# The end of a graph-attention kernel: the last node blocks in groups of 4, 2 and 3, and two steps of the pending work for each pair of edges in the last three blocks

## The chip, the cores and the metric

The kernel runs on one core of a Trainium2 chip. The metric is the device time in microseconds (us) of one execution. PE is the matrix engine (TensorE, with PEld for its weight loads), DVE the vector engine, ACT the scalar engine, POOL GpSimd, which here issues the indirect gathers and scatters, and SP the engine whose queue carries the plain DMAs. Each engine takes its instructions strictly in the order in which the program lists them, and waits on semaphores that the others raise.

## The reference, cut to what matters

There are 6250 nodes of 512 floats and 100,000 edges, each with eight bias values. A layer norm is followed by attention with 8 heads over each node's incoming edges, a projection and a residual, and then by a small "ALU" pipeline: three matrix layers on features decoded from each node's second layer norm, of which two outputs per position are used.

```python
q, k, v = x @ Wq + bq, x @ Wk + bk, x @ Wv + bv      # x is layer-normed, 8 heads of 64
logits = einsum('ehd,ehd->eh', q[rows] * scale, k[cols]) + att_bias
att = softmax of logits over the edges of one row
y = segment_sum(att[:, :, None] * v[cols], rows)
x1 = x + (y @ Wo + bo)
...
h = relu(relu(x_ge @ W0 + b0) @ W1 + b1) @ W2 + b2    # once with Wa, once with Ws
...
out = layernorm(x1) + x1, with a few columns (128 to 160) added to from rounded h
```

(The lines are shortened from the reference; the last stage selects between the two pipelines by flags in columns 0 to 2 of the normed row.)

## The kernel before, in words

The edges are sorted by node on the chip, keys and values of all nodes are written to a table in HBM, and then a main loop handles 49 blocks of 128 nodes (`NB` = 49). Block numbers in this document are places in the loop's order, 0 to 48. A node sits on one partition; a block has as many edge slots as its busiest node has edges (`CAP`): 16 slots in block 45, and 10, 9 and 8 in the last three blocks, 46, 47 and 48. A block of more than 12 slots is taken in two parts.

For each pair of slots POOL gathers two rows of keys and values (`kv`, 4 KB for each partition and slot, 11 buffers of a pair each), and DVE multiplies the keys by the block's query and sums by head (`dots`, L813 and L814, 2.4 us for a pair). After the last pair of a part comes the softmax (L742 to L760, DVE and ACT). The weighting of the values and their sum belong to `sums` (L1091): DVE multiplies the values of most pairs by the softmax's weights (L824), ACT those of the last one or two full pairs (L822, eight short instructions for a slot), and PE adds all slots up with a multiplication by the identity into `p_y` (L1104). `sums` is put off: it is written into the program after the `dots` of the next part's first pair, so for block b it stands behind the first pair of block b+1.

What follows on the sums is a generator for each block, `part_end` (L1058): it divides by the softmax's denominator (L785 to L789), turns the result (L832 on PE, L835 on ACT), multiplies by Wo (L841, L842 on PE), adds the residual and takes mean and variance (L845 to L848 on DVE). The query of the next block is a generator too (`project`: L802 on PE, L804 on ACT, L808 and L809 on PE). When all blocks of a group have come so far, the group's ALU pipeline, the generator `alu` (L850), is put into the list `alus`:

- an "E" step: the square root on ACT (L855) between two table loads, then the norm on DVE and ACT (L858 to L868);
- a "D" step: decoding on DVE (L874 to L887), and a turn on PE (L891); then `fT` is copied out on DVE (L895);
- ten "P" steps on PE and ACT: five matrix products L905 with ACT's relu L907, five outputs of the second layer L918 (13 products) with L920, and then the third layer L925 (5 products). All of them have 128 times the number of blocks in the group as their columns;
- two more "D" steps: `yf` is copied out on DVE (L928), turned back on PE (L932), and DVE makes the outputs (L938 to L973). POOL then scatters one block's rows at a time (L794).

The order of all this is the program's own and fixed when it is built: the scheduler is switched off (`manual_schedule`). `pump` (L1003) is called once ahead of each pair's `dots`: it moves every generator in `going` (`part_end`, `project`) by one step, and `alus` by up to `n` steps of the kinds allowed. `alu_steps` (L1014) does the latter alone; it is called after each softmax for up to four "P" steps. Groups are taken from `alus` one after the other. The groups have 4 blocks; `heads_of` (L1044) cuts the end into groups of 2, 2 and 1: blocks 44 and 45, 46 and 47, and 48. Scatters are held back while gathers remain (`HOLD`, L1130), so all those of blocks 40 to 48 stand behind the last gather. After the last block, the loop at L1160 pumps until nothing is left.

Of the kernel before, what the change touches and what calls it, by code (L numbers as in the profile page):

```python
# [20 lines left out]
P = 128  # L21
# [7 lines left out]
GB = 4  # L29
# [14 lines left out]
def gnn_ffn_kernel(  # L44
# [4 lines left out]
    N, D = x.shape  # L49
# [6 lines left out]
    NB = -(-N // P)  # L56
# [52 lines left out]
    def gather(dst_t, table, idx):  # L109
        nc.gpsimd.indirect_dma_start(  # L110
            out=dst_t, out_offset=None, in_=table,
            in_offset=bass.IndirectOffsetOnAxis(ap=idx, axis=0))
# [111 lines left out]
    def fetch_keys(b):  # L224
        C = CAP[ORDER[b]]
        t, nbuf = ("0", 1) if b == 0 else ("", LA + 3)
        kg = pre.tile([P, C + 1], F32, tag="kg" + t, name="kg", bufs=nbuf)
        gather(kg, words, pos_i[:, ORDER[b]:ORDER[b] + 1])
        st[b] = dict(kg=kg)

    def read_keys(b):
        C = CAP[ORDER[b]]
        t, nbuf = ("0", 1) if b == 0 else ("", LA + 3)
        f0 = pre.tile([P, 1], F32, tag="f0", name="f0", bufs=2)
        neg, eid = decode(st[b]["kg"], 1, C, f0, t, nbuf, ids=nid[:, b:b + 1])
        rec = pre.tile([P, C, ROW], F32, tag="rec" + t, name="rec", bufs=min(nbuf, LA + 2))
        st[b].update(neg=neg, rec=rec, eid=eid)
# [10 lines left out]
    def fetch_recs(n, last):  # L248

        while fetched[0] < n and fetched[1] is not None and fetched[1][0] <= last:  # L250
            b, s = fetched[1]
            gather(st[b]["rec"][:, s, :], rec_d, st[b]["eid"][:, s:s + 1])
            fetched[:] = fetched[0] + 1, next(wanted, None)
# [484 lines left out]
    def softmax(lg, rec, neg, m0):  # L738


        n = lg.shape[1]
        nc.vector.scalar_tensor_tensor(lg, lg, SCALE, rec[:, :, 1:], op0=OP.mult, op1=OP.add)  # L742
        nc.vector.tensor_tensor(lg, lg, neg[:, :, None].to_broadcast([P, n, H]), op=OP.add)
        m = ap_.tile([P, H], F32, tag="m", name="m", bufs=4)
        nc.vector.tensor_reduce(m, lg.rearrange("p c h -> p h c"), AX.X, OP.max)
        if m0 is None:
            nc.vector.tensor_scalar(m, m, FLOOR, None, op0=OP.max)
        else:
            nc.vector.tensor_tensor(m, m, m0, op=OP.max)
        nc.vector.tensor_tensor(lg, lg, m[:, None, :].to_broadcast([P, n, H]), op=OP.subtract)  # L750
        nc.scalar.activation(lg, lg, AF.Exp)  # L751
        turn_[1] ^= 1
        p_ps = pp[:, turn_[1] * P:turn_[1] * P + n * H].rearrange(
            "p (c h) -> p c h", h=H)
        nc.scalar.copy(p_ps, lg)
        cor = None
        if m0 is not None:
            cor = ap_.tile([P, H], F32, tag="cor", name="cor", bufs=3)
            nc.vector.tensor_tensor(cor, m0, m, op=OP.subtract)
            nc.scalar.activation(cor, cor, AF.Exp)  # L760
        return m, cor, p_ps
# [36 lines left out]
    def project(xg, s_):  # L798

        pt = ops.tile([P, KC, P], F32, tag="tr", name="tr", bufs=1)  # L800
        for c in range(KC):
            nc.tensor.transpose(pt[:, c, :], xg[:, D + c * P:D + (c + 1) * P], ident)  # L802
        xT = o2.tile([P, KC, P], F32, tag="xT", name="xT", bufs=2)
        nc.scalar.copy(xT, pt)  # L804
        yield
        q = s_["q"] = ops.tile([P, D], F32, tag="q", name="q")
        for c in range(KC):
            nc.tensor.matmul(q, xT[:, c, :], wq[:, c, :], start=(c == 0), stop=False)  # L808
        nc.tensor.matmul(q, ones3, bq3, start=False, stop=True)  # L809

    def dots(kvt, n, q, dot, s):
        k = kvt[:, :n, :D]
        nc.vector.tensor_tensor(k, k, q[:, None, :].to_broadcast([P, n, D]), op=OP.mult)  # L813
        nc.vector.tensor_reduce(  # L814
            dot[:, s:s + n, :], k.rearrange("p s (h d) -> p s h d", h=H), AX.X, OP.add)
# [164 lines left out]
    def fetch_nodes(b):  # L980
        if b - 4 in ends:
            run(ends.pop(b - 4))
        xg = ap_.tile([P, 2 * D], F32, tag="xg", name="xg", bufs=4)
        gather(xg, xx_d, nid[:, b:b + 1])
        st[b]["xg"] = xg
# [13 lines left out]
    def store(n=1):  # L999
        for _ in range(n):  # L1000
            stores.pop(0)[1]()

    def pump(kinds="", n=1):  # L1003

        last[1] += 1
        for g in list(going):
            if next(g, True):
                if g in going:
                    going.remove(g)
        alu_steps(kinds, n)  # L1010
        if stores and stores[0][0] + last[0] <= last[1]:
            store()

    def alu_steps(kinds, n):  # L1014

        while alus and n > 0 and kind[0] in kinds:
            kind[0] = next(alus[0], None)
            if kind[0] is None:
                alus.pop(0)
                kind[0] = "P"  # L1020
            n -= 1

    def run(g):

        while alus and g in alus and g is not alus[0]:
            run(alus[0])
        for _ in g:
            pass
        if g in alus:
            kind[0] = "P"  # L1030
        for l in (going, alus):
            if g in l:
                l.remove(g)
# [7 lines left out]
                LASTR if ORDER[g + j] == NB - 1 else P), g))  # L1041


    heads_of = list(range(0, NB - 5, GB)) + [NB - 5, NB - 3, NB - 1]  # L1044
    head = {b: max(g for g in heads_of if g <= b) for b in range(NB)}

    def start_group(g):
        i = heads_of.index(g)
        n = (heads_of + [NB])[i + 1] - g
        t, nbuf = ("", 2) if i < len(heads_of) - 2 else (str(i), 1)  # L1050
        if i > 1 and nbuf > 1 and heads_of[i - 2] in groups:
            run(groups.pop(heads_of[i - 2])[2])
            while stores and stores[0][2] <= heads_of[i - 2]:
                store()
        groups[g] = [o2.tile([P, n if t else GB, D], F32, tag="x1" + t, name="x1", bufs=nbuf),
                     o2.tile([P, GB, 2], F32, tag="mv", name="mv", bufs=4), None]
# [55 lines left out]
    for b in range(NB):  # L1112
        C = CAP[ORDER[b]]
        s_ = st[b]
        rec, q = s_["rec"], s_["q"]
        parts = -(-C // PART)
        m = None
        for i in range(parts):
            s0, s1 = C * i // parts, C * (i + 1) // parts
            n_ = s1 - s0  # L1120
            dot = ap_.tile([P, n_, H], F32, tag="dot", name="dot", bufs=2)
            kvs = []
            for s in range(s0, s1, 2):
                n = min(2, s1 - s)
                kvt = kvp.tile([P, 2, 2 * D], F32, tag="kv", name="kv")
                for j in range(n):
                    gather(kvt[:, j, :], kv_d, rec[:, s + j, 0:1].bitcast(I32))
                kvs.append((kvt, n, s - s0))
                done = sum(SLOTS[:b]) + s + n
                if done > HOLD:  # L1130
                    last[0] = 1000
                fetch_recs(FIRST + (TOTAL - FIRST) * done // (TOTAL - LAST), b + LA)
                if s == s0 and i == 0:
                    if b + LA + 2 < NB:
                        fetch_keys(b + LA + 2)
                    if b + 1 < NB:
                        fetch_nodes(b + 1)
                if s == s0 + 2 and i == 0 and b + 1 < NB:
                    pj = project(st[b + 1]["xg"], st[b + 1])
                    going.insert(0, pj)  # L1140


                k = len(kvs) - 1
                pump("" if k < 2 else "D" if s + 2 >= s1 else "DE" if k == 2 else "DEP")
                dots(kvt, n, q, dot, s - s0)
                if s == s0:
                    for f in waiting:
                        f()
                    waiting.clear()
                if s == s0 + 2 and i == parts - 1 and b + LA + 2 < NB:  # L1150
                    read_keys(b + LA + 2)
            m, cor, p_ps = softmax(dot, rec[:, s0:s1], s_["neg"][:, s0:s1], m)
            waiting.append(partial(sums, b, i, parts, dot, cor, p_ps, kvs, n_))
            alu_steps("P", min(4, len(kvs) - 1))
        if b + 1 < NB:
            run(pj)
    for f in waiting:
# [149 lines left out]
```

## Time and profile before

| what | us |
|---|---|
| median of 3 runs (lowest, highest) | 3293.85 (3280.11, 3300.85) |
| the profiled execution, its own time | 3294.45 |
| its span, first to last instruction | 3292.6 |
| main loop's last gather of keys and values issued by POOL (ends) | 3166.9 |
| last `p_y` product of block 48 ends | 3212.5 |
| last DVE instruction (L973 of block 48) ends | 3276.6 |
| busy: PE, DVE, ACT, POOL | 2066.8, 2021.9, 880.8, 1708.2 |
| mean granted clock of PE | 0.800 |

How it is read: times in the trace are us from the span's start. A timeline line has the start, the busy time, the engine, the source line, the operation, what it writes and reads, how many instructions are merged in it, and in brackets how long the engine sat idle before and what released it. A product of 512 columns in f32 is two records of 0.43 us each at PE's full clock. In a table of stages, "PEclk" is the share of PE's clock that was granted. In the records the clock is at either 1.0 or 0.5.

### The profile page before, as it was taken

How to read it: one execution, taken by the hardware profiler on the slowest of the kernel's cores; microseconds unless marked ns; L12 is line 12 of the kernel's file. 1: busy time of each engine (PE TensorE's matmuls, PEld its weight loads, DVE VectorE, ACT ScalarE, POOL GpSimd, SP SyncE). 2: the span in 40 equal slices, each digit the busy share in tenths (PEclk: the TensorE clock that was granted, in tenths of full speed). 3: DMA queues.
4: the chain of work that ended last, by engine and by line, in shares of the span. 5: the costliest groups of instructions: out<-in, count | busy, mean ns of one | idle time of the engine just before them, and what ended most of it. 6: DMA issues, size and time to landing. Idle time of an engine off the chain costs nothing.

```text
span 3292.6 us, 20197 instructions
## 1 busy us (share of the span) xinstructions
PE 2066.8 (63%) x4853; PEld 888.6 (27%) x4853; DVE 2021.9 (61%) x3593; ACT 880.8 (27%) x2656; POOL 1708.2 (52%) x1858
## 2 busy tenths in 40 slices
PE   7887318644556647466477485757757557566586
PEld 3443103311222222122222132222323222222233
DVE  9887000176747655575677558767677766666672
ACT  6443003121212122131232222323223232222232
POOL 2011760274666555655665646665666646656530
PEclk9999658866777878778788788787978879778797
DMA  8443113465555554655565646665666646556530
GB/s 272 170 155 108 25 16 128 142 215 189 171 172 182 161 180 154 200 162 167 186 193 171 200 150 197 196 194 177 195 196 194 203 128 201 186 163 193 164 116 17
DMA packets 193964, 542.30 MB, mean 165 GB/s; under 512 B 51831, under 2 KB 53174, under 8 KB 193841
## 3 DMA queue, kind: packets, MB, share of 16 engines
q0 software_dynamic: 154416, 464.27, 44.9%
q1 hardware_dynamic: 39425, 76.67, 6.7%
q8 instruction: 42, 0.69, 0.1%
q14 instruction: 81, 0.66, 0.1%
HBM read 472.60 MB, written 68.22 MB: 164 GB/s over the span
## 4 chain that ended last, share of the span: by engine, by line
PE 40%; DVE 18%; another core or an unknown queue 17%; issue 16%; ACT 5%; POOL 2%; DMA 1%; SPq 0%; POOLq 0%; DVEq 0%; ACTq 0%
PE p_y L1104 13%; PE pm L468 8%; DVE kv L813 5%; PE pm L918 4%; PE q L808 4%; PE pm L841 3%; DVE dot L814 3%; ACT kv L822 3%; DVE kv L824 3%; PE pm L905 2%; PE p L925 2%; DVE key L143 1%; POOL kv L110 1%; DVE key L144 1%
## 5 line engine op out<-in xcount | busy, mean ns | idle before, releaser
L110 POOL DMA_INDIRECT kv<-kv_d,rec x804 | 760.7, 946 | 763.7 <-PE p_y L1104 346.3
L1104 PE MATMUL p_y<-kv,ident 128*128 128x512 f32 x1608 | 832.9, 674 | 383.5 <-issue 169.6
L110 POOL DMA_INDIRECT rec<-rec_d,eid x804 | 762.8, 949 | 245.1 <-issue 236.6
L813 DVE TENSOR_TENSOR kv<-kv,q 128x1024 f32<-128x1024 f32 (+1 forms) x425 | 489.9, 1153 | 200.1 <-DMA kv<-kv_d,rec 127.5
L1104 PEld LDWEIGHTS p_y<-kv,ident 128*128 128x128 f32 x1608 | 335.3, 215 | 852.2 <-issue 554.2
L814 DVE TENSOR_REDUCE dot<-kv 128x16 f32<-128x1024 f32 (+1 forms) x425 | 493.8, 1162 | 79.2 <-ACT kv L822 42.1
L822 ACT ACTIVATE kv<-kv,dot 128x64 f32<-128x64 f32 x1568 | 387.0, 336 | 31.8 <-issue 31.8
L808 PE MATMUL q<-wq,xT 128*128 128x512 f32 x392 | 215.4, 700 | 271.3 <-issue 185.8
L824 DVE TENSOR_TENSOR kv<-kv,pp 128x1024 f32<-128x1024 f32 (+1 forms) x327 | 352.7, 1137 | 0.0
L841 PE MATMUL pm<-wo,yT 128*128 128x512 f32 x392 | 213.4, 695 | 204.4 <-issue 125.5
L468 PE MATMUL pm<-wv,xnT 128*128 128x512 f32 (+1 forms) x392 | 190.7, 622 | 17.5 <-issue 17.5
L468 PE MATMUL pm<-wk,xnT 128*128 128x512 f32 (+1 forms) x392 | 189.3, 625 | 0.0
L804 ACT COPY xT<-tr 128x512 f32<-128x512 f32 x49 | 28.7, 585 | 594.9 <-remote 333.3
L808 PEld LDWEIGHTS q<-wq,xT 128*128 128x128 f32 x392 | 83.3, 224 | 374.0 <-issue 283.9
L841 PEld LDWEIGHTS pm<-wo,yT 128*128 128x128 f32 x392 | 85.6, 227 | 315.8 <-issue 231.3
L835 ACT COPY yT<-tr 128x512 f32<-128x512 f32 x49 | 28.7, 585 | 482.3 <-remote 262.6
L766 DVE TENSOR_REDUCE den<-dot 128x8 f32<-128x64 f32 (+6 forms) x91 | 24.7, 272 | 198.5 <-ACT dot L751 166.8
L479 ACT COPY kvt<-pm 128x512 f32<-128x512 f32 (+1 forms) x98 | 57.1, 583 | 323.3 <-remote 133.7
L417 DVE RECIPROCAL rstd<-rstd 128x7 f32<-128x7 f32 (+4 forms) x9 | 1.7, 186 | 214.5 <-ACT rstd L413 158.6
L110 POOL DMA_INDIRECT xg<-xx_d,nid x49 | 46.2, 943 | 160.6 <-DMA kv_d<-kvt 128.9
L905 PE MATMUL pm<-fT,w 8*128 8x512 f32 (+2 forms) x140 | 91.0, 774 | 52.1 <-DVE fT L895 28.0
L920 ACT ACTIVATE h<-pm,b 128x512 f32<-128x512 f32 (+2 forms) x70 | 44.1, 633 | 285.3 <-PE pm L918 115.4
(257 smaller groups left out, 2129.1 us busy)
## 6 DMA issues: line engine op xcount, KB each, us to landing
kv_d<-kvt SPq DMA_DIRECT2D x48, 512.0 KB
rec<-rec_d,eid POOLq DMA_INDIRECT x804
kv<-kv_d,rec POOLq DMA_INDIRECT x804
xt<-in_x_dram SPq DMA_DIRECT2D x48, 256.0 KB
xx_d<-xt SPq DMA_DIRECT2D x48, 256.0 KB
xx_d<-xn SPq DMA_DIRECT2D x48, 256.0 KB
rec_d<-R SPq DMA_DIRECT2D x3, 882.0 KB
bt<-in_edge_attr_dram SPq DMA_DIRECT2D x3, 686.0 KB
```

Of the source, the lines that this page charges most:

```text
L110: nc.gpsimd.indirect_dma_start(out=dst_t, out_offset=None, in_=table, in_offset=bass.IndirectOffsetOnAxis(ap=idx, axis=0))
L468: nc.tensor.matmul(pm[:r], xnT[b][:, c, :r], wkv[nm_][:, c, :], start=(c == 0), stop=(i == 1 and c == KC - 1))
L808: nc.tensor.matmul(q, xT[:, c, :], wq[:, c, :], start=(c == 0), stop=False)
L813: nc.vector.tensor_tensor(k, k, q[:, None, :].to_broadcast([P, n, D]), op=OP.mult)
L814: nc.vector.tensor_reduce(dot[:, s:s + n, :], k.rearrange("p s (h d) -> p s h d", h=H), AX.X, OP.add)
L822: nc.scalar.mul(v[:, i, h], v[:, i, h], p[:, s + i, h:h + 1])
L824: nc.vector.tensor_tensor(v, v, p_ps[:, s:s + n, :, None].to_broadcast([P, n, H, DK]), op=OP.mult)
L841: nc.tensor.matmul(pm, yT[:, c, :], wo[:, c, :], start=(c == 0), stop=False)
L905: nc.tensor.matmul(pm[:, :nt], w0[:, c * P:(c + 1) * P], fT[:, t0:t1], start=True, stop=True)
L918: nc.tensor.matmul(pm[:, :nt], w, h1[:, k, :nt], start=(i == 0), stop=(i == len(terms) - 1))
L925: nc.tensor.matmul(p3[:, :nt], w2[:, c, :], h2[:, c, :nt], start=(c == 0), stop=(c == NC4))
L1104: nc.tensor.matmul(p_y, ident, kvt[:, j, D:], start=(done_ == 0), stop=(done_ == n_ - 1))
```

## The change

It does two things, both of which only concern the program after the first pair of block 46.

1. `heads_of` ends with two heads instead of three, so that blocks 46, 47 and 48 are one group of three. Their ALU pipeline runs once with 384 columns, instead of once with 256 and once with 128.
2. In the last three blocks `pump` is called twice ahead of each pair, each time with up to two ALU steps of any kind. `part_end` and `project` so move by two steps for each pair. Before, the first pair allowed no ALU step, the second and last few kinds, and the others one step. After the softmax of these blocks up to four ALU steps of any kind may follow, instead of "P" alone.

```diff
-    heads_of = list(range(0, NB - 5, GB)) + [NB - 5, NB - 3, NB - 1]
+    heads_of = list(range(0, NB - 5, GB)) + [NB - 5, NB - 3]
...
-        t, nbuf = ("", 2) if i < len(heads_of) - 2 else (str(i), 1)
+        t, nbuf = ("", 2) if i < len(heads_of) - 1 else (str(i), 1)
...
                 k = len(kvs) - 1
-                pump("" if k < 2 else "D" if s + 2 >= s1 else "DE" if k == 2 else "DEP")
+                if b >= NB - 3:
+                    pump("DEP", 2)
+                    pump("DEP", 2)
+                else:
+                    pump("" if k < 2 else "D" if s + 2 >= s1 else "DE" if k == 2 else "DEP")
                 dots(kvt, n, q, dot, s - s0)
...
             waiting.append(partial(sums, b, i, parts, dot, cor, p_ps, kvs, n_))
-            alu_steps("P", min(4, len(kvs) - 1))
+            alu_steps("P" if b < NB - 3 else "DEP", min(4, len(kvs) - 1))
```

The second line gives the last group a tile of its own (of 3 blocks instead of one of 2 and one of 1), which leaves the memory used the same.

What the two programs list on PE, one beside the other, from the second part of block 45 on (x counts products; "ALU" with the group's blocks; the third layer is L925):

| before | after |
|---|---|
| ALU 40-43: L905 x3 | ALU 40-43: L905 x5, L918 x4 |
| `p_y` 45, second part, x8; L802 and `q` of 47 | `p_y` 45 x8; L802 of 47; L918 x4; `q` of 47 |
| ALU 40-43: L905 x2, L918 x6 | ALU 40-43: L918 x5, L925 x5, L932 |
| L832 of 45 | L832 of 45; Wo of 45 |
| `p_y` 46 x10; L802 of 48; Wo of 45; `q` of 48 | `p_y` 46 x10; L802 of 48; ALU 44-45: L891, L905 x1; `q` of 48 |
| ALU 40-43: L918 x7, L925 x5; L832 of 46 | ALU 44-45: L905 x4, L918 x4; L832 of 46; L918 x4; Wo of 46; L918 x5, L925 x5, L932 |
| `p_y` 47 x9; Wo of 46; L932 | `p_y` 47 x9; L832 and Wo of 47 |
| `p_y` 48 x8; then L832 and Wo of 47 and 48 among ALU 44-45 | `p_y` 48 x8; L832 and Wo of 48 |
| ALU 46-47; ALU 48 | ALU 46-48, 384 columns |

On DVE, the copy `yf` (L928) of ALU 40-43 stands before in the middle of block 47's pairs, and after behind the second pair of block 46, ahead of the other three. L928 of ALU 44-45 stands before at the end, and after ahead of block 47's last pair (its single slot). POOL's gathers keep their order.

## The prediction

> **What bounds the kernel now.** I read the stage table first, to see where the changed part lies and which engine is busy there; then the timelines of DVE, ACT and PE from 3120 us on; then the chain of waits for the end. Main loop and sort stand in the same order in both programs, so only what follows about 3127 us can differ: 165 of 3292.6 us.
>
> Stages from the table. Columns: stretch, its length, busy us (and instructions) of PE, PEld, DVE, ACT and POOL, PE's granted clock, share of the DMA engines' time, GB/s.
>
> ```profile
> 3121.00:3157.00 36.00, 30.86 (x69) 12.45 (x69) 35.10 (x44) 9.54 (x27) 17.23 (x18) 0.91 0.48 147
> 3157.00:3203.00 46.00, 36.70 (x92) 14.91 (x90) 24.39 (x51) 13.39 (x46) 11.09 (x12) 0.93 0.25 84
> 3203.00:3213.00 10.00, 9.24 (x21) 4.17 (x21) 7.46 (x21) 7.76 (x22) 0.37 (x1) 0.79 0.10 39
> 3213.00:3277.00 64.00, 48.53 (x172) 30.12 (x171) 17.22 (x82) 23.07 (x45) 3.95 (x5) 0.79 0.05 17
> ```
>
> Until 3157 DVE is busy 35.1 of 36 us. From there PE and DVE take turns, and the last 64 us are one chain: the ends of blocks 47 and 48, then three ALU pipelines in a row, DVE 17 us busy and PE 49. The DVE timeline shows the hand-overs that cost:
>
> ```profile
> 3164.49 0.69 DVE L789 TENSOR_TENSOR y<-p_y,den 128x512 f32<-128x512 f32 x1 [6.75 <-PE p_y L1104]
> ...
> 3183.54 0.68 DVE L928 COPY yf<-p 8x512 f32<-8x512 f32 x1 [1.09 <-PE p L925]
> ...
> 3195.95 0.19 DVE L948 TENSOR_TENSOR ys<-py,b 128x32 f32<-128x32 f32 x1 [8.60 <-PE py L932]
> ...
> 3276.43 0.20 DVE L973 TENSOR_TENSOR x<-x,de 128x33 f32<-128x33 f32 x1
> ```
>
> With 1.67 and 2.02 us of smaller waits, DVE stands still 20 us between 3121 and 3203. L928 of the group of four costs it 1.09 us only, because it stands where the pipeline is already through. From ACT and PE:
>
> ```profile
> 3149.07 0.69 ACT L920 ACTIVATE h<-pm,b 128x512 f32<-128x512 f32 x1 [4.29 <-issue]
> 3156.78 1.26 ACT L920 ACTIVATE h<-pm,b 128x512 f32<-128x512 f32 x2 [7.03 <-PE p_y L1104]
> ```
>
> ```profile
> 3146.64 1.02 PE L918 MATMUL pm<-h,w1lm 128*128 128x512 f32 x2
> 3152.17 7.03 PE L1104 MATMUL p_y<-kv,ident 128*128 128x512 f32 x16
> 3203.76 8.79 PE L1104 MATMUL p_y<-kv,ident 128*128 128x512 f32 x16 [7.85 <-DVE kv L824]
> 3242.75 4.83 PE L905 MATMUL pm<-fT,w 8*128 8x256 f32 x10 [0.51 <-DVE fT L895]
> 3255.28 2.33 PE L925 MATMUL p<-h,w 128*8 128x256 f32 x10
> ```
>
> ACT takes at 3156.78 what PE had done at 3147.66: 9 us late, while gathers run at 0.48 of the DMA engines' time. PE's results reach ACT late in such stretches.
>
> **The change, part by part.** All times are of the one profiled execution (3294.45 us, span 3292.6); the difference found is then put on the median of 3293.85, 0.6 below.
>
> *The group of three at the end.* Before, from the end of block 48's last product (3212.55) to the end of the last L973 (3276.63): 64.1 us. After: L789 0.75; turn on PE 0.65; copy on ACT 0.5; Wo 3.95 (3.60 and 0.38 in the rows of 3191); L845 to L848 1.6; the root 0.35, its table load done before; L858 to L863 0.33 and three of L866 0.86; L874 to L887 between 1.25 (two blocks) and 2.1 (four), taken 1.5; turn 0.5; fT 0.55: 11.5 us. PE's 23 products: with 256 columns they took from 3242.75 to 3257.61, 14.9 us; at full clock 46 records of 0.2155 are 9.9, so 5.0 went to a slow clock at the start and to one wait for ACT. With 384 columns 46 x 0.323 = 14.9, and the same 5.0: 19.9. Then yf to L973, 3.2 for two blocks: 3.3. Sum 34.7, **29.4 less**. Three scatters instead of one stand at the end; POOL's pitch for them is 1.27 (3261.11, 3262.38): **2.5 more**. The 16 us behind the last L973 stay.
>
> The Trainium skill ("TensorE: Matmul & The Clock Gate", "What's actually happening") says that the array runs at half rate only for about the first 3.4 us of sustained work; by it the extra would be 1.7, and the sum 3.3 lower. But the granted clock was 0.53 from 3243 to 3252 and 0.99 only from 3252 to 3262: 9 us at half rate, which are 4.5 lost. I keep the row.
>
> *Two steps for each pair.* It moves the rest of ALU 40-43 into block 46's first two pairs, and ALU 44-45 into blocks 46 and 47, both ahead of work that DVE could do. Nothing is computed more; what counts is where L928 comes.
>
> First stall. PE's list is now L905 x5, L918 x4, p_y, L802, L918 x4, q, L918 x5, L925 x5 before L928 can go. The first three L905 end at 3127.7 as before. Two more at half clock with their relus on ACT, and two outputs of L918 at 1.9 each: 3135.9 (before, p_y began at 3127.6). p_y 7.0, L802 0.4, L918 x4 3.7, q 3.9, L918 x5 4.3, L925 4.4: **3159.7**. DVE has done pair 1, three weightings, L845 to L848, L1063 and pair 2 by 3132.7, and stands at L928 for **27 us**; behind it in its queue are three pairs of block 46, the softmax that ACT waits for, all weightings of blocks 46 to 48. Before, it had gone on at once.
>
> From 3159.7: yf and what follows 3.65 (0.6 + 0.83 + 2.25), L1067 to L789 1.84, three pairs 7.15, softmax 1.3, L845 to L848 1.56, ALU 44-45's E step 1.5, one pair and L766 2.65, one weighting 1.15: block 46's p_y can start at 3180.5 (before 3152.2). PE: 20 records of 0.43 are 8.6. PE had waited 9 us; p_y of 48, which came after a wait of 7.85, took 8.79 where 16 records otherwise take 7.03, so 1.8 more: 3191. Turns and fT 1.3, L905 and q 4.6, four L905 2.3, two L918 outputs 1.8, L832 0.5, two outputs 1.8, Wo 4.0, the last output and L925 4.3: L928 of ALU 44-45 at **3211.5**. DVE got there at 3200.8: second stall, 10.7. In front of it, fT waited 6.8 for the turn that stands behind p_y.
>
> Then 3.3 for its outputs, block 47's single slot and softmax 2.7, L845 to L848 1.6, one pair, L766 and a weighting 3.8: p_y 47 starts at 3222.9, 18 records and 1.8 for the clock, 3232.5. L789 0.7, two pairs 4.8, softmax, ACT's exp and L766 1.85, a weighting 1.15: p_y 48 starts at 3241 and ends at **3248.1**, 35.6 later than before.
>
> Sum: +35.6 - 29.4 + 2.5 = **+8.7**.
>
> *Late signals.* ALU 40-43 is now a chain of some eight hand-overs from PE to ACT, in the stretch of 3130 to 3155 where gathers run. Before, one of them was 9 us late and DVE had other work. The largest row of this kind near by is L835 at 3114.40, whose turn on PE ended at 3095.6: 19. So between 0 and 19 per stall; I take 6, below the 9 just seen, because the gathers pause while DVE stands. Elsewhere gathers are over (block 48's last three pairs excepted, 8 us of them beside p_y 46, where nobody waits).
>
> Costed at nothing: one pipeline's two table loads on ACT go away, which ran under L925 before (3255.9 to 3258.8). The scatters' waits block no gather, since they all stand behind the last one.
>
> **Forecast:** +8.7 + 6 = +14.7, so a span of 3307 and, on the median, **3309 us**.
>
> **The rivals.**
>
> *Not slower: PE's clock stays up.* Of the sum, 5.0 at the tail and 1.8 for each of p_y 46 and 47 are half clock. If PE is granted the full clock there, 8.6 go, and without late signals the sum is 0: 3294. It decides from 8.7 us on. For it: the clock changes from stage to stage (0.96, 0.77, 0.88, 0.96, 0.50 from 3167 to 3243). Against it: the same page's section "HAM oscillation" says that each idle wait of over 3.4 us throttles the array again, and the change makes PE wait 9 and 11 us where it waited 7.85 at most from 3157 on; the row of 8.79 agrees.
>
> *Slower by over 1%: late signals twice.* If two of the hand-overs in ALU 40-43 come 12 to 19 us late, DVE stands for it, +8.7 + 25 = +34: 3328. For it: the 19 us of L835. Against it: 1 such in the last 200 us of before, and the gathers end when their buffers are full.
>
> *The moved work is hidden.* If DVE stood no longer than its 20 us of before, only the tail would count: -26.9, 3267. Against it: the two L928 stand ahead of their own pairs, in an engine that goes in order.
>
> **How the numbers follow.** A difference of 1% (33 us) is about what a measurement of this kernel can tell from no change; the three runs before spread over 21 us. Forecast's case (3300 to 3326) 0.57, full clock (3280 to 3300) 0.20, hidden (below 3280) 0.07, late signals twice (above 3326) 0.16. Even the hidden case is only 0.8%, so faster by over 1% gets 0.04, same 0.80, slower 0.16. Range for 8 in 10: 3286 to 3329.
>
> **What would show it.** In the new trace: L928 of 512 columns with some 25 us of idle time before it, released by L925; the one of 256 columns with 10; block 46's first L824 near 3180, last p_y ending near 3248; one ALU with 384 columns of 20 us on PE; three scatters, 1.27 apart. Wrong if DVE idles less than 15 us at the first L928, if p_y 48 ends before 3235, or if ACT's L920 of that group wait over 12 us each.

## The result, and the profile after

| | before | after |
|---|---|---|
| median of 14 runs each, us | 3284.55 | 3310.56 |
| lowest, highest | 3235.48, 3300.85 | 3277.37, 3322.52 |
| the profiled execution: own time, span, mean clock | 3294.45, 3292.6, 0.800 | 3283.61, 3281.8, 0.797 |
| the end stretch: from the start of the copy `fT` (L895) of ALU 40-43 to the span's end | 171.5 (from 3121.1) | 193.0 (from 3088.9) |

The change made the kernel slower: ratio 1.011, 95% interval 1.0065 to 1.0154; by the medians 26 us. Here and below, ratios leave out the runs of a kernel that lie more than 1.5% above its fastest (in `e4_warm` one of 4376 us), and medians do not, so that the two can differ. The two profiled executions show the opposite, 10.8 us less. They are misleading as a whole: everything ahead of that `fT` is listed in the same order in both programs, and it was 32.2 us shorter in the profile after. So I compare the end stretch alone, which is 193.0 - 171.5 = **21.4 us longer** (differences are from unrounded marks). That is at the lower end of the interval (1.0065 x 3284.55 is 21.3 more); whether anything else was added can't be told from spreads of 45 and 65 us.

Stages of the kernel after, in the same columns as before (stretch, length, busy us of PE, PEld, DVE, ACT, POOL, clock, DMA share, GB/s):

```profile
3089.00:3125.00 36.00, 32.30 (x61) 12.58 (x62) 11.21 (x15) 11.06 (x27) 18.07 (x19) 0.76 0.50 155
3125.00:3171.00 46.00, 30.84 (x72) 12.05 (x70) 30.34 (x63) 11.28 (x29) 12.46 (x14) 0.81 0.29 96
...
3238.00:3263.00 25.00, 22.06 (x49) 10.45 (x49) 2.76 (x16) 5.81 (x10) 0.00 (x0) 0.74 0.00 1
```

In the first 36 us DVE is busy 11.2 where it was busy 35.1 in the matching stretch before. Its timeline in the kernel after says what it stands at:

```profile
3088.86 0.68 DVE L895 COPY fT<-pf 8x512 f32<-8x512 f32 x1 [3.34 <-PE pf L891]
...
3131.62 0.68 DVE L928 COPY yf<-p 8x512 f32<-8x512 f32 x1 [30.84 <-PE p L925]
...
3164.31 0.41 DVE L895 COPY fT<-pf 8x256 f32<-8x256 f32 x1 [7.19 <-PE pf L891]
3186.47 0.41 DVE L928 COPY yf<-p 8x256 f32<-8x256 f32 x1 [13.27 <-PE p L925]
...
3259.83 0.55 DVE L928 COPY yf<-p 8x384 f32<-8x384 f32 x1 [21.81 <-PE p L925]
3263.01 0.26 DVE L973 TENSOR_TENSOR x<-x,de 128x99 f32<-128x99 f32 x1
```

The first two L928 cost DVE 30.84 and 13.27 us; before, the first of them cost 1.09. The last has nothing behind it but its own outputs. PE in the same kernel:

```profile
3094.40 2.07 PE L905 MATMUL pm<-fT,w 8*128 8x512 f32 x2 [0.78 <-ACT h L907]
...
3102.09 2.08 PE L918 MATMUL pm<-h,w1mm 128*128 128x512 f32 x2
...
3152.52 10.25 PE L1104 MATMUL p_y<-kv,ident 128*128 128x512 f32 x20 [8.26 <-DVE kv L824]
...
3197.77 10.66 PE L1104 MATMUL p_y<-kv,ident 128*128 128x512 f32 x18 [10.55 <-DVE kv L824]
...
3217.05 8.70 PE L1104 MATMUL p_y<-kv,ident 128*128 128x512 f32 x16 [2.59 <-DVE kv L824]
...
3238.08 6.76 PE L905 MATMUL pm<-fT,w 8*128 8x384 f32 x10 [0.64 <-DVE fT L895]
```

PE in turn waits 8.26, 10.55 and 2.59 us for DVE's weighted values, and works at half rate for a part of what follows: 16 records of a `p_y` took 7.03 where PE had been busy, 8.70 here. And two records of L905 took 2.07; in the kernel before, at full rate, two took 1.12.

### The profile page after: what moved, and what is told of

Its sections match the earlier page's. It is cut to its first block, busy times and chain, and to the rows that moved or that the text cites. A ratio compares the mean times of both kernels' runs of the same rounds, so it can differ in the third digit from the quotient of the medians.

```text
span 3281.8 us, 20060 instructions
## 1 busy us (share of the span) xinstructions
PE 2058.5 (63%) x4807; PEld 882.8 (27%) x4807; DVE 2019.3 (62%) x3567; ACT 875.9 (27%) x2642; POOL 1707.2 (52%) x1858
## 3 DMA queue, kind: packets, MB, share of 16 engines
q0 software_dynamic: 154416, 464.27, 45.4%
## 4 chain that ended last, share of the span: by engine, by line
PE 34%; another core or an unknown queue 22%; DVE 18%; issue 16%; ACT 6%; POOL 3%; DMA 1%; POOLq 0%; DVEq 0%; SPq 0%; ACTq 0%
PE p_y L1104 11%; PE pm L468 8%; DVE kv L813 4%; PE pm L918 4%; PE pm L841 3%; DVE dot L814 3%; ACT kv L822 3%; PE q L808 3%; DVE kv L824 2%; PE pm L905 2%; PE p L925 1%; POOL kv L110 1%; POOL rec L110 1%; DVE key L143 1%
## 5 line engine op out<-in xcount | busy, mean ns | idle before, releaser
L1104 PE MATMUL p_y<-kv,ident 128*128 128x512 f32 x1608 | 820.2, 666 | 359.0 <-issue 155.2
L808 PE MATMUL q<-wq,xT 128*128 128x512 f32 x392 | 224.1, 724 | 355.8 <-issue 224.5
L804 ACT COPY xT<-tr 128x512 f32<-128x512 f32 x49 | 28.7, 586 | 702.6 <-remote 473.1
L808 PEld LDWEIGHTS q<-wq,xT 128*128 128x128 f32 x392 | 87.1, 234 | 464.1 <-issue 327.5
L1067 DVE TENSOR_TENSOR y<-y,p_y 128x512 f32<-128x512 f32 x42 | 28.7, 683 | 198.3 <-remote 140.8
L835 ACT COPY yT<-tr 128x512 f32<-128x512 f32 x49 | 28.7, 585 | 411.4 <-remote 190.1
L905 PE MATMUL pm<-fT,w 8*128 8x512 f32 (+2 forms) x130 | 92.6, 841 | 59.3 <-DVE fT L895 35.6
```

Of the source, the lines that this page charges most:

```text
L905: nc.tensor.matmul(pm[:, :nt], w0[:, c * P:(c + 1) * P], fT[:, t0:t1], start=True, stop=True)
L1104: nc.tensor.matmul(p_y, ident, kvt[:, j, D:], start=(done_ == 0), stop=(done_ == n_ - 1))
```

## The experiments

Three theories. **A**, mine: DVE goes in order, and the two `yf` copies stand ahead of its own pairs, so that it waits for a whole PE pipeline each time. **B**: the group of three is what costs. **C**: PE's clock, halved after the new waits, makes the loss. Each kernel is "before" or "after" with one edit. Three chips were used: one for `e1` to `e4`, one for `e5` to `e8`, one for `e9` to `e12`; each ratio is to runs of the kernel before on the same chip, whose medians were 3283.49, 2639.25 and 3305.64 us. No end stretch of the kernel before was profiled on the second and third chip; the row "before" is the profile of the result. All marks of the table are us from the start of the copy `fT` of ALU 40-43 in the one profiled execution of that kernel.

| kernel | end stretch | `p_y` 46 starts | `p_y` 47 | `p_y` 48 starts, ends | last L973 ends | ratio (95%) |
|---|---|---|---|---|---|---|
| before | 171.5 | 31.1 | 63.0 | 82.7, 91.5 | 155.5 | |
| after | 193.0 | 63.7 | 108.9 | 128.2, 136.9 | 174.4 | 1.011 (1.0065-1.0154) |
| `e1_groups` | 170.2 | 40.3 | 67.7 | 87.4, 96.3 | 151.8 | 0.997 (0.9939-1.0001) |
| `e2_steps` | 190.7 | 64.6 | 109.9 | 129.2, 137.9 | 174.9 | 1.0061 (1.0025-1.0098) |
| `e3_yf_later` | 170.9 | 55.8 | 84.4 | 107.3, 116.1 | 152.5 | 1.0004 (0.9972-1.0036) |
| `e4_warm` | 185.3 | 62.6 | 108.4 | 125.0, 132.1 | 166.9 | 1.0069 (1.0039-1.0099) |
| `e5_groups_warm` | 154.1 | 28.4 | 55.9 | 75.6, 82.7 | 135.7 | 0.9972 (0.9963-0.9981) |
| `e6_last_block` | 162.0 | 28.6 | 60.6 | 80.1, 90.1 | 143.6 | 0.9988 (0.998-0.9997) |
| `e7_last_block_warm` | 155.9 | 28.6 | 60.5 | 80.1, 87.2 | 137.5 | 0.9976 (0.9967-0.9985) |
| `e8_yf_early` | 178.3 | 30.1 | 75.8 | 101.5, 110.4 | 159.9 | 1.0052 (1.0036-1.0067) |
| `e9_after_again` | 191.4 | 61.2 | 108.9 | 128.3, 137.0 | 172.9 | 1.0089 (1.0054-1.0124) |
| `e10_groups_again` | 165.2 | 31.1 | 63.0 | 82.7, 91.4 | 146.8 | 0.9985 (0.9955-1.0014) |
| `e11_steps_again` | 190.0 | 63.8 | 109.1 | 128.4, 137.1 | 174.1 | 0.9999 (0.9973-1.0026) |
| `e12_yf_later_again` | 179.1 | 56.1 | 92.0 | 115.2, 124.1 | 160.6 | 1.0024 (0.999-1.0059) |

### The halves of the change: `e1_groups`, `e10_groups_again`, `e2_steps`, `e11_steps_again`

The groups alone are the kernel before with the change's two lines on `heads_of` and `len(heads_of)`.

> Only the groups of 4, 2 and 3; one step for each pair as before. I measure the end stretch, from the start of the copy fT (L895) of ALU 40-43 to the end of the span: 171.5 us in the profile before, 192.9 in the profile after. Theory A (DVE stands at the two yf copies of the double steps, in front of its own pairs): without the double steps nothing stands still, ALU 44-45 stays at the end and ALU 46-48 follows it at once; from 3239 of before, 3.8 for its preparation, 20 to 22 on PE, 3.5, and 2.5 for two more scatters: end stretch 163 to 167, total 4 to 9 us less than before. Rival B (the group of three is what costs, its products wait for all of block 48): end stretch 180 or more.

> The groups of 4, 2 and 3 alone, again. On the chip without late copies: 3 to 6 us below before (0.9977 to 0.9989), end stretch 158 to 161.

In `e10_groups_again` all marks up to the end of `p_y` 48 are those of before to 0.1 us, and the last L973 ends 8.7 earlier; two more scatters at the end leave 171.5 - 165.2 = 6.3 of it. `e1_groups` is 170.2, because there a hand-over in ALU 40-43 came late (ACT's L920 started at 3180.22 on a result that PE had finished at 3174.64), PE stood behind it, and DVE got the sums of block 46 later (L789 waited 11.37 us, not 6.75). By itself the group of three saves 6 us in one profile and 1 in the other, and costs nothing: **B falls** as the cause of the loss. By the total times the gain can't be told from none on either chip. DVE's `yf` copies in `e10_groups_again`:

```profile
3194.01 0.68 DVE L928 COPY yf<-p 8x512 f32<-8x512 f32 x1 [1.09 <-PE p L925]
...
3246.20 0.41 DVE L928 COPY yf<-p 8x256 f32<-8x256 f32 x1 [8.11 <-PE p L925]
...
3274.87 0.55 DVE L928 COPY yf<-p 8x384 f32<-8x384 f32 x1 [20.99 <-PE p L925]
```

The double steps alone, with the heads of before, are "after" with the two lines of `heads_of` and `len(heads_of)` put back.

> Only the double steps in the last three blocks, with the groups of 2, 2 and 1 as before. Theory A: the two stalls at yf (30.8 and 13.3 us in the profile after) stand as in the changed kernel, the last product for block 48 ends some 137 us after that fT, and two pipelines follow instead of one: end stretch 192 to 200, total 20 to 30 us above before. Rival B (the group of three costs): end stretch near 171.

> The double steps alone, with groups of 2, 2 and 1, again. On the chip without late copies: 22 to 28 us above before, at most 3 from the changed kernel, end stretch 186 to 192.

Their stretches are 190.7 and 190.0, the stalls at the first two L928 30.92 and 13.12, 31.0 and 13.2: 18.5 to 19.2 us of the loss are in the steps. In total time the first is slower by 0.6%, the second shows no difference, where 18.5 us would be 0.56%. By the medians of all runs it is 9 us slower (3314.74 against 3305.64). The traces agree with each other and the totals don't; I go by the traces and leave that total as a miss.

The halves do not add up. The groups alone gain, yet the change is 1 to 3 us longer than the steps alone (193.0 and 191.4 against 190.7 and 190.0). Beside the steps the group of three no longer gains: the last L973 ends at 174.4 and 172.9 with it, at 174.9 and 174.1 without, and two more scatters stand behind it. With the steps alone the pipeline of blocks 46 and 47 follows block 48's Wo at once, at full rate:

```profile
3273.96 0.38 PE L842 MATMUL pm<-bo,sT 66*128 66x512 bf16 x1
3274.18 0.38 PE L891 MATMUL pf<-ident,ft 128*8 128x128 f32 x2
3275.06 3.21 PE L905 MATMUL pm<-fT,w 8*128 8x256 f32 x10 [0.51 <-DVE fT L895]
```

In `e11_steps_again`, shown here, the products of that pipeline took 11.5 us and those of block 48 another 9.9. The one pipeline of 384 columns took 21.7, more than half of it at half rate.

### The place of the copies: `e3_yf_later`, `e12_yf_later_again`

The groups and double steps of "after", but the D steps (decoding, the `yf` copies and the outputs) only behind the softmax, where DVE has done its pairs:

```diff
                 if b >= NB - 3:
-                    pump("DEP", 2)
-                    pump("DEP", 2)
+                    pump("EP", 2)
+                    pump("EP", 2)
```

> The changed kernel, but in the last three blocks the D steps (decoding, yf copy, outputs) may only follow the softmax of a block, no longer stand ahead of a pair; E and P steps stay doubled. Theory A: DVE does all pairs of block 46 before it waits for yf, so the first stall shrinks to under 12 us (it waits up to 15 at L1067 for block 45's sum instead) and the second nearly goes; the last product for block 48 ends 20 to 25 us earlier: end stretch 165 to 175. Rival C (the slow clock of PE and late signals cost, wherever DVE waits): end stretch 185 to 195.

> The changed kernel with its D steps only behind a block's softmax, again. On the chip without late copies: 3 to 8 us above before, some 20 below the changed kernel, end stretch 166 to 171.

This takes all of the loss back (170.9, 22 us less than "after"), in the repeat 12 to 14 us (179.1). DVE of `e3_yf_later`:

```profile
3130.52 0.69 DVE L1067 TENSOR_TENSOR y<-y,p_y 128x512 f32<-128x512 f32 x1 [13.34 <-PE p_y L1104]
...
3146.72 0.68 DVE L928 COPY yf<-p 8x512 f32<-8x512 f32 x1 [5.63 <-PE p L925]
...
3204.31 0.41 DVE L928 COPY yf<-p 8x256 f32<-8x256 f32 x1
```

The copies cost 5.63 us and nothing, in place of 30.84 and 13.27; L948, behind each, waits another 4.08 and 3.73 for PE's turn. **A holds**, but not for the whole delay: `p_y` 48 ends 21 us earlier than in "after" (116.1, not 136.9) and still 25 later than before (91.5). That the stretch is nevertheless that of before comes from the shorter tail. A new stall takes part of the copies' place: the sums of block 45 still come late, because PE does nine products of the pipeline ahead of them, and L1067 waits 13.34. No run leaves PE's share of the moved work where it was while the copies stay late, so what of the 25 us is PE's order is not shown.

In total times the repeat and the change can be compared on one chip: the medians are 3299.55 (`e12_yf_later_again`) and 3332.54 (`e9_after_again`). The repeat has the same two waits (14.02 and 5.63), and is longer in block 47: `p_y` 46 ends only 0.9 later (67.9 and 67.0), but then ACT's copy L835 started 3.1 us after the turn it copies (0.04 in the first run), PE stood 3.66 and did Wo in 6.34 at half rate instead of 3.70, `fT` of ALU 44-45 waited 6.71 instead of 0.97, and `p_y` 47 started 7.6 later.

### A's stall by itself: `e8_yf_early`

The groups, and in the last two blocks single calls of two steps with everything allowed from the second pair on, so that the `yf` copy of ALU 40-43 stands ahead of pairs of block 47 (the kernel before allows no ALU step ahead of the first two pairs of a part):

```diff
-                pump("" if k < 2 else "D" if s + 2 >= s1 else "DE" if k == 2 else "DEP")
+                if b >= NB - 2:
+                    pump("" if k < 1 else "DEP", 2)
+                else:
+                    pump("" if k < 2 else "D" if s + 2 >= s1 else "DE" if k == 2 else "DEP")
...
-            alu_steps("P", min(4, len(kvs) - 1))
+            alu_steps("P" if b < NB - 2 else "DEP", min(4, len(kvs) - 1))
```

> Groups of 4, 2 and 3, and single calls of pump; in blocks 47 and 48 all ALU steps are allowed, two for a call, from the second pair on. There the yf copy of ALU 40-43 stands behind block 47's second pair, while PE ends that pipeline about 62 us after fT as before. Theory A, without any doubled step of the sums: DVE stands 25 to 30 us at that copy, block 47's p_y starts 20 us later than before (83 instead of 63 us after fT), end stretch 172 to 185. If it is the doubling of part_end that costs: a wait under 10 us and 160 to 167.

DVE of this kernel:

```profile
2529.92 0.68 DVE L928 COPY yf<-p 8x512 f32<-8x512 f32 x1 [24.13 <-PE p L925]
...
2562.24 0.41 DVE L895 COPY fT<-pf 8x256 f32<-8x256 f32 x1 [7.35 <-PE pf L891]
...
2594.90 0.41 DVE L928 COPY yf<-p 8x256 f32<-8x256 f32 x1 [11.98 <-PE p L925]
```

With up to two steps for a pair instead of four, a copy ahead of DVE's own pairs costs 24.13 us. The last L973 ends 24 us later than in `e5_groups_warm` on the same chip, which has idle products besides, and 16 later than in `e6_last_block`, which has none; the kernel is 0.5% slower than before. So the place of the copy alone makes such a stall, without doubled calls.

### PE's clock: `e4_warm`

"After", with products that keep PE busy in its waits. Their results are never read:

```diff
+    def warm_pe(n):
+        pm = ops.tile([P, D], F32, tag="mm", name="pmw")
+        for _ in range(n):
+            nc.tensor.matmul(pm, ident, wq[:, 0, :], start=True, stop=True)
...
+        if b in (46, 47, 48):                   # in sums, ahead of p_y
+            warm_pe({46: 5, 47: 11, 48: 2}.get(b, 0))
...
+        if n == GB - 1:                         # in alu, ahead of the turn pf
+            warm_pe(5)
```

> The changed kernel with idle products on PE whose results nobody reads (128x512, identity by Wq, into a free buffer of mm): 5 ahead of block 46's p_y, 11 ahead of 47's, 2 ahead of 48's and 5 ahead of the last pipeline's turn, in stretches where PE stands idle. They keep its clock up. Rival C: p_y of 46, 47 and 48 take 8.8, 7.9 and 7.0 instead of 10.25, 10.66 and 8.70, the last pipeline's products 16 instead of 21.8: 11 to 12 less, end stretch about 181. Theory A alone (DVE's order is all of it): no less than 190. Both can hold; the sum of them is then what was missing in the forecast.

It is 7.7 us shorter (185.3), 6.1 by the repeat of "after". PE of `e4_warm`:

```profile
3218.91 9.71 PE L1096 MATMUL pmw<-wq,ident 128*128 128x512 f32 x22 [0.54 <-DVE ys L950]
3228.94 7.99 PE L1113 MATMUL p_y<-kv,ident 128*128 128x512 f32 x18 [0.31 <-DVE kv L824]
...
3258.56 4.46 PE L1096 MATMUL pmw<-wq,ident 128*128 128x512 f32 x10
3264.72 4.80 PE L907 MATMUL pm<-fT,w 8*128 8x384 f32 x10 [0.64 <-DVE fT L897]
3269.45 1.65 PE L920 MATMUL pm<-h,w1mm 128*128 128x384 f32 x2
```

`p_y` 47 takes 7.99 in place of 10.66, `p_y` 48 7.13 in place of 8.70, the first layer of the last pipeline 4.80 in place of 6.76. But `p_y` 46 took 11.89, not the 8.8 expected: PE stood 4.04 between the idle products and it, and the rate was half again. The last pipeline's products took 19.2, not 16. The first stall stays 30.17. So the clock is a part of the loss, but the smaller: **C holds for 6 to 8 us**, and alone it does not bring the kernel back to before.

### Versions that might beat both: `e5_groups_warm`, `e6_last_block`, `e7_last_block_warm`

The groups alone with idle products (6 ahead of `p_y` 48, 5 ahead of the turn `pf` of the last pipeline):

> Groups of 4, 2 and 3 with single steps as before, and idle products on PE (6 ahead of block 48's p_y, 5 ahead of the last pipeline's turn; nobody reads them). The groups alone gave an end stretch of 170.2 us in a profile with one late hand-over of 5 us, so about 165 without it. Theory A with the clock: 1.7 less at p_y of 48 and 2.5 to 5 less in the last pipeline: end stretch 158 to 163, or 5 more with such a late hand-over; total 8 to 13 below before. If the clock is nothing: 165 to 170.

The groups, and the double "EP" steps of `e3_yf_later` in the last block alone, without and with idle products:

```diff
+                if b >= NB - 1:
+                    pump("EP", 2)
+                    pump("EP", 2)
+                else:
+                    pump("" if k < 2 else "D" if s + 2 >= s1 else "DE" if k == 2 else "DEP")
...
-            alu_steps("P", min(4, len(kvs) - 1))
+            alu_steps("P" if b < NB - 1 else "DEP", min(4, len(kvs) - 1))
```

> Groups of 4, 2 and 3; double steps only in block 48, and there D steps only behind the softmax, so that the yf copy of ALU 40-43 stands where PE is through (62 us after fT), and ALU 44-45 begins beside block 48's sum instead of after it. Theory A: no DVE wait over 10 us for yf of ALU 40-43, last p_y ends 92 to 95 us after fT as before, and the two pipelines end earlier: end stretch 156 to 163, total 8 to 15 below before. If double steps cost wherever they stand: above 171.

> The same with idle products on PE, 3 ahead of block 48's p_y and 5 ahead of the last pipeline's turn. Theory A with the clock: 3 to 5 less than without them, end stretch 152 to 160. If the clock is nothing: as without them.

All three are faster than before, and `e5_groups_warm` has the lowest median: 2631.84 us against 2639.25, ratio 0.9972 (0.9963 to 0.9981). That is 0.28%, small but clear of none; from `e7_last_block_warm` it can't be told apart. Steps moved into the last block gain nothing beyond it: with idle products in both, the last L973 ends at 137.5 with them (`e7_last_block_warm`) and at 135.7 without. They put new waits in front of DVE: in `e6_last_block` L845 waits 6.03 and 8.21 us, L789 5.60 and `fT` 5.87. What the groups alone are worth on this chip was not run; between `e6` and `e7` the idle products make 6.1 us of the last L973's end.

### Once more: `e9_after_again`

"After", unchanged, on the third chip, beside `e10` to `e12`.

> The changed kernel once more, beside its two halves on the same chip. The last four runs fell on a chip where the kernel before took 2639 us with a spread of 0.1%, and where no copy on ACT came late behind PE; there, the end stretch of before must be about 163.5 (their stretches less their differences: 154.1 + 7.4, 162.0 + 3.2, 155.9 + 6.3, 178.3 - 13.7). Theory A on such a chip: the two stalls remain, end stretch 187 to 193, total 24 to 29 us above before (1.009 to 1.011). If late hand-overs made up the loss: under 10 us above before. On a chip like the first: ratio 1.005 to 1.015.

Stretch 191.4 (193.0 in the first profile of after), stalls 28.82, 8.55 and 14.44, ratio 1.0089 (1.0054 to 1.0124). The end stretch of this kernel repeats within 2 us, where its total times on this chip spread over 45 (3300.62 to 3345.78).

## Why the prediction was right, and where it was not

The forecast was 3309 us, 15 more than before; by the end stretch it was 21, by the medians 26. That 3309 lies within 2 us of the measured median is luck: the loss was 11 us larger, and the kernel before 9 us faster in the result (3284.55) than in the three runs forecast from (3293.85). All times below are from the start of `fT` of ALU 40-43, predicted and measured in the profile after.

**The first stall: right.** L928 was to be reached at 38.6 after 27 us of standing; it came at 42.8 after 30.84. The 4.2 are one term of PE's list. "Two more at half clock ... and two outputs of L918 at 1.9 each" put the start of block 45's `p_y` at 14.8; it was 19.5. The last L905 ended at 13.3, not 11 (14.8 less two outputs), since the half rate already held for the second product. And 1.9 is an output (two products) at full rate; behind the half-rate L905 one product took 1.9 to 2.08 in three of four, and the four took 6.4 instead of 3.8. From that `p_y` on, the sum (23.8) was half a us long.

**From the first copy to `p_y` 46: right.** 20.8 predicted, 20.9 measured. This is DVE's own work, taken from durations of rows.

**The second stall: right.** 10.7 predicted, 13.27 measured; `fT` waited 7.19 (6.8). PE again: from the end of `fT` to L928 19.2 predicted, 21.75 measured. The query of block 48 (L808) took 5.40 where the row used had 3.60, at half rate behind the wait.

**`p_y` 47 and 48: small misses.** I gave 1.8 for the clock to 46 and 47, and nothing to 48. `p_y` 46 took 10.25 (10.4 predicted), 47 took 10.66 (9.6), 48 took 8.70 (7.1). The end of `p_y` 48 came 45.4 us later than before, not 35.6.

**The group of three: right in its length.** From there to the last L973 34.7 predicted, 37.5 measured; PE's products took 21.7, not 19.9: L905 alone ran 6.76 at half rate, and L918 stayed at half rate to 3251. The row of before that I kept over the page's 3.4 us (the Trainium skill, "TensorE: Matmul & The Clock Gate", "What's actually happening") was nearer, and still too short: the half rate lasted 12 to 13 us from 3238 on. The three scatters follow 1.28 and 1.27 apart, as said (POOL of the kernel after):

```profile
3263.55 0.97 POOL L794 DMA_INDIRECT out_dram<-x,nid  x1 [71.38 <-DVE x L973]
3264.83 0.97 POOL L794 DMA_INDIRECT out_dram<-x,nid  x1 [0.30 <-issue]
```

**Late signals: the step that failed.** "So between 0 and 19 per stall; I take 6." In the profile after, this chain has one late hand-over. ACT of the kernel after:

```profile
3128.78 0.69 ACT L920 ACTIVATE h<-pm,b 128x512 f32<-128x512 f32 x1 [8.81 <-remote]
```

The result it takes was finished on PE at 3127.19, 1.59 earlier, and the ten records of L925 behind it ran on in 4.46 without a gap, so it cost nothing. The base sum of +8.7 was +21.4 in truth, the 12.7 more being 4.2 in the first stall, 2.9 in the second, 2.7 at `p_y` 47 and 48, 2.8 in the tail and 0.1 between. Most of each is PE's half rate. So the forecast came near because a term for late signals, which hardly occurred, stood where a larger term for the clock belonged. The direction and the mechanism (the order on DVE) were right for the reason given, the size by luck.

**The rivals.** "PE's clock stays up" is the opposite of what happened; `e4_warm` shows what part of it would have been worth, 6 to 8 us, and that even then the stretch is 13.8 above before. "The moved work is hidden" is refuted by the stalls of 30.84 and 13.27. "Late signals twice" did not occur in the stretch of either profile of the change; that such waits exist is seen in `e1_groups` and `e12_yf_later_again`.

## What to carry to other kernels

In an engine that goes in order, a step that waits for another engine's pipeline belongs behind the engine's own ready work: two copies of 0.7 and 0.4 us cost 44 us of standing here. Moving them gave back 13 to 21 us at the end of the last sum, since other waits moved up into their place. Work that is pulled forward must be judged by where its last hand-over lands in each queue, not by whether the engine that computes it has gaps. And where runs spread by more than the effect, compare a stretch that starts behind the unchanged part.

## What the runs showed of the hardware that was not expected

**Hand-overs from PE to ACT can come tens of us late, and on one chip they never did.** ACT's copy of a turn (L804) starts 0.04 to 0.09 us after PE's turn ends in most cases. In the profile before, 14 of the 49 started 1.5 to 35 us late. One of them, first ACT, then PE:

```profile
1185.12 0.58 ACT L804 COPY xT<-tr 128x512 f32<-128x512 f32 x1 [46.85 <-remote]
```

```profile
1149.54 0.60 PE L802 MATMUL tr<-ident,xg 128*128 128x128 f32 x4
```

The turn ended at 1150.14, the copy began at 1185.12, and PE stood 35.6 us behind it. ACT's waits in the profile before, and those of `e5_groups_warm` on the second chip (us in total, times, longest):

```profile
ACT xT L804 <- remote: 333.3, 12, 46.9
ACT yT L835 <- remote: 262.6, 15, 42.3
```

```profile
ACT xT L804 <- PE tr L802: 394.0, 49, 21.3
ACT yT L835 <- PE tr L832: 218.9, 34, 18.6
```

On the second chip all 49 copies began 0.04 to 0.09 us after the turn, and the kernel before took 2639 us (2636.61 to 2643.51) instead of 3283 to 3306: a fifth less, with a mean clock of 0.870 in `e5_groups_warm` against 0.800. In the two places of before that I compared (L835 at 3114.40, L920 at 3156.78) the gathers paused within 3 us of the stall's end; that they are the cause is not shown. Loading of instructions does not explain them: in 11 of the 14 waits of L804 no packet of an instruction queue was moved. Why one chip does this and another does not stays open.

**Products with 8 rows of weights let the clock fall.** In `e4_warm`, 4.46 us of idle products at full rate and no idle time over 0.64 us stand ahead of the last pipeline, yet the rate fell to half within the ten records of L907 (8 x 128 weights; L905 in the other kernels), and stayed there until 3274.6:

```profile
3258.00:3264.00 6.00, 5.42 (x16) 2.11 (x14) 4.05 (x15) 3.54 (x6) 0.00 (x0) 1.00 0.00 0
3264.00:3269.00 5.00, 4.31 (x11) 1.75 (x10) 0.55 (x1) 2.68 (x5) 0.00 (x0) 0.88 0.00 0
3269.00:3274.00 5.00, 5.00 (x8) 2.52 (x8) 0.00 (x0) 1.16 (x2) 0.00 (x0) 0.50 0.00 0
```

In these stages PE is busy 5.42, 4.31 and 5.00 of 6, 5 and 5 us, and the granted clock goes 1.00, 0.88, 0.50. By the Trainium skill ("TensorE: Matmul & The Clock Gate", "HAM oscillation") the throttle returns after idle gaps of more than some 3.4 us; here it returned without one.

The 14 profiles together say what counts. In all of them the granted clock changes on a raster of 3.41 us. For each such stretch the share was taken in which PE was busy with anything but products with 8 rows of weights. It was at least 0.78 in the stretch ahead of each of the 1231 returns to full rate, and at most 0.53 ahead of each of the 1245 falls to half. Those with 8 rows do not help: in the profile before, PE was busy with L905 alone through one whole stretch at full rate, and had half the rate in the next:

```profile
1469.80:1473.19 3.39, 3.39 (x8) 0.95 (x6) 3.22 (x5) 2.05 (x3) 2.69 (x3) 1.00 0.83 266
1473.20:1476.60 3.40, 1.73 (x3) 0.83 (x3) 3.37 (x7) 0.63 (x2) 2.59 (x3) 0.50 0.63 197
```

Few columns of weights do no harm: in the kernel after, L925 (128 x 8) alone filled 3128.1 to 3131.5, and the rate stayed full until 3134.9. The last pipeline of the kernel after fits this: through the 6.76 us of L905 the rate stayed at half, and it came back at 3251, 6.2 us after the first L918. All this is read from the records; no run changed the number of rows alone.
